# q and k projected in 32-column tiles and turned by VectorE, exp per head from PSUM, rotary tables scaled ahead, layernorm sums on half arrays

## The chip, the cores and the metric

The kernel runs on one core of one Trainium2 chip. The core has TensorE (PE) for matrix products, VectorE (DVE), ScalarE (ACT) and GpSimd (POOL) for elementwise work, and SyncE (SP), which issues the transfers here. TensorE reads its operands from the on-chip memory SBUF and writes its products to PSUM, eight banks of 128 partitions by 512 float32. The metric is the device time of one execution in microseconds.

## The reference, cut to what matters

Input x has 2 sequences of 2048 tokens with 128 features. Four residual steps follow one another; each reads the layernorm of x.

```python
x = x + attn_a(ln(x))            # full attention, softmax over the first token axis
x = x + ffn(ln(x))               # two layers, below
x = x + attn_b(ln(x))            # token weights from q/k statistics and a small convolution
x = x + ffn(ln(x))

def layer(x, ...):               # ffn is two of these
    q, k, v = split(shift_token(x) @ wqkv, 3)      # 8 heads of 64
    q, k = l2norm(q) * q_scale, l2norm(k) * k_scale
    q = q * cos * scale + rotate_half(q) * sin * scale
    k = k * cos / scale + rotate_half(k) * sin / scale
    x = x + local_attention(q, k, v) @ wo          # windows of 64, each sees itself and the one before
    h = layernorm(shift_token(x)) * lg + lb
    a, g = split(h @ w1 + b1, 2)
    return x + (a * gelu(g)) @ w2 + b2
```

The windowed attention is run over 2 sequences, 2 uses of ffn, 2 layers and 16 blocks of 128 tokens: 128 blocks in all, each of 8 heads. All arithmetic is float32; only the mask is bfloat16.

## The kernel before

**How it is put together.** The kernel does not issue instructions directly. `op(engine, cost, fn, r, w, claim)` notes an operation with the engine that runs it, an assumed cost in microseconds, and what it reads and writes. `Program.run` then walks through a list schedule with these costs, hands out buffers from fixed pools (`sizes`, with the eight PSUM banks as pool `p1`), and issues the operations in the resulting order. That order is fixed on every engine; only semaphores decide when each instruction starts. So the costs in the code shape the order, and the chip sets the times.

**The stages.** Tokens are loaded in 8 chunks of 512. `first_norm` and `first_attention` do the full attention of each sequence. Then `Block.tick` runs the ffn steps: 16 blocks of layer 0, with layer 1 of the same sequence 6 ticks behind, the next sequence following. After every fourth block comes `feed_forward` on 512 tokens. `token_weights` does the third step of a sequence.

**A block of windowed attention** (`Attention.block`). The state `s` lies with features on partitions and tokens along the free axis. The steps with their lines:

- L498, L499: a table of 4 x 64 trigonometric values for each token is loaded, and POOL multiplies it by the q and k scales.
- L503: q and k are projected, each one product of 128 tokens by 512 columns into one PSUM bank; L507 does v. A float32 product is two passes in the profile. Tokens now lie on partitions.
- L510, L514: SP copies halves of v to a buffer with shifted windows.
- L523: ACT squares q and k; L524, L525: DVE multiplies them by the two halves of the table, the second with the halves of each head exchanged; L527: DVE sums the squares over each head.
- L528: POOL adds the two products. L530 to L533: POOL clips the sums of squares, ACT takes the inverse root by Ln and Exp, and `newton` refines it in four small POOL operations. L536: POOL multiplies the rotated q and k by it.
- L543, L545 (through `transposes`, L389): eight 128x128 transposes on TensorE bring features back to partitions; ACT copies q (L544) and k into a ring of three blocks (L546).
- L557, L573: scores of the two windows and two head parities, each in a 64x64 quadrant of the array. A masked bfloat16 product starts each sum.
- L581, L582: DVE takes the row maxima and subtracts them; L583: ACT takes the exponential of all 1024 columns; L587, L588: DVE sums rows and inverts; L593: POOL scales the weights.
- L600, L601: eight more transposes and their copies; L612: the product with v by 64-column tiles; L618: ACT copies; every second block, L624 projects the output and L630, L631 add it to the state.

**Layernorm** (`center`, L453 to L463) works on 128 features by 512 tokens. A product with `meanw`, a matrix of 1/128, puts the mean of each token on all 128 partitions (L457); DVE subtracts (L458), ACT squares, a second such product gives the variance (L460), and ACT takes the inverse root by Ln and Exp (L461, L462). It is called 56 times: 16 times by `state_norm`, 32 times by `feed_forward`, 8 times by `token_weights`.

## Time and profile before

| | us |
|---|---|
| median of three runs | 1736.16 |
| lowest and highest of them | 1735.68, 1736.17 |
| profiled execution | 1736.7 |
| span of its instructions | 1734.9 |

The mean granted TensorE clock of the profiled execution is 0.986. Line numbers (L503) are those of the kernel before. In a row of groups, the count after x is the number of records, and a group can be split by the buffer that its tile got. Busy time is the union of the instructions' times; the idle time is that of the engine just before the group's instructions. In a timeline, neighbouring instructions of one kind are merged into one row with their number. Some matmul records can be missing.

### The profile page before, as it was taken

Reading aid. Unit: us, or ns where it says so; the run is one execution under the profiler, and the core shown is the slowest. Engines: PE = TensorE matmul, PEld = TensorE weight load, DVE = VectorE, ACT = ScalarE, POOL = GpSimd, SP = SyncE. Lnnn points to the kernel's source line nnn. Section 1 sums busy time; section 2 is a strip of 40 time slices with the busy share of each in tenths; the row PEclk is TensorE's granted clock in tenths of the full one; section 3 lists DMA queues with packets and bytes.
Section 4 is the critical chain, followed back from the end, with each engine's and each line's share of the span. In section 5 each row is a group of like instructions: output and inputs, shape, how many; then the busy total and the mean of one; then the engine's idle time right before and its main releaser. Section 6 shows DMA issues by size and latency. Waiting matters only on the chain.

```text
span 1734.9 us, 35224 instructions
## 1 busy us (share of the span) xinstructions
PE 1660.6 (96%) x13638; PEld 996.6 (57%) x13638; DVE 1277.5 (74%) x2095; ACT 1112.4 (64%) x2029; POOL 1196.2 (69%) x1548
## 2 busy tenths in 40 slices
PE   8999998999999999899999998999999999999996
PEld 4444446665656565456666664565656665665654
DVE  6323258787778886888788797887788888888663
ACT  6444456666677666667766765767676776766663
POOL 4000029789788785688699686869699788987762
PEclk9999999999999999899999999999999999999998
DMA  5000001111111110111111111111111111111110
GB/s 156 0 0 1 0 22 41 32 41 41 37 29 44 38 26 22 31 29 40 35 38 41 32 26 31 32 35 38 38 41 44 44 43 44 33 49 40 32 32 7
DMA packets 50603, 59.98 MB, mean 35 GB/s; under 512 B 6955, under 2 KB 33925, under 8 KB 50437
## 3 DMA queue, kind: packets, MB, share of 16 engines
q1 hardware_dynamic: 50436, 57.73, 13.3%
q8 instruction: 108, 1.77, 0.4%
q14 instruction: 59, 0.48, 0.1%
HBM read 23.11 MB, written 2.10 MB: 15 GB/s over the span
## 4 chain that ended last, share of the span: by engine, by line
PE 67%; DVE 14%; POOL 13%; ACT 3%; issue 3%; DMA 0%; POOLq 0%; SPq 0%; DVEq 0%; ACTq 0%
PE pp L389 10%; PE pp L660 8%; PE pp L503 8%; PE pp L446 6%; PE pp L435 6%; PE pp L612 6%; PE pp L624 5%; PE pp L573 4%; PE pp L507 4%; PE pp L685 4%; POOL arena L528 3%; DVE b_m L581 2%; DVE arena L582 2%; POOL arena L593 2%; POOL arena L536 2%
## 5 line engine op out<-in xcount | busy, mean ns | idle before, releaser
L593 POOL TENSOR_TENSOR arena<-arena,b_m 128x512 f32<-128x512 f32 x226 | 230.3, 1040 | 102.1 <-DVE b_m L588 84.3
L389 PE MATMUL pp<-ident,arena 128*128 128x128 f32 x1792 | 250.8, 279 | 23.4 <-POOL arena L593 10.7
L389 PEld LDWEIGHTS pp<-ident,arena 128*128 128x128 f32 x1792 | 206.8, 143 | 112.8 <-issue 56.2
L503 PE MATMUL pp<-wqkv,b_s 128*128 128x512 f32 x512 | 258.2, 607 | 0.2 <-POOL b_s L483 0.2
L528 POOL TENSOR_TENSOR arena<-arena 128x1024 f32<-128x1024 f32 x90 | 212.6, 2364 | 29.9 <-DVE arena L525 27.9
L536 POOL TENSOR_TENSOR arena<-arena,b_n 128x1024 f32<-128x1024 f32 x107 | 203.8, 1906 | 3.1
L581 DVE TENSOR_REDUCE b_m<-pp 128x4 f32<-128x512 f32 x256 | 165.1, 679 | 47.0 <-PE pp L573 45.0
L660 PE MATMUL pp<-b_c,w 128*128 128x512 f32 (+1 forms) x384 | 179.5, 618 | 16.3 <-POOL b_c L656 10.9
L524 DVE TENSOR_TENSOR arena<-pp,b_tab 128x512 f32<-128x512 f32 x214 | 145.9, 683 | 61.4 <-ACT arena L523 33.3
L601 ACT COPY arena<-pp 128x512 f32<-128x512 f32 x232 | 130.0, 589 | 89.0 <-PE pp L389 83.8
L482 POOL TENSOR_TENSOR b_s<-b_c,b_c 64x512 f32<-64x512 f32 x16 | 20.3, 1266 | 210.5 <-ACT b_c L462 210.3
L523 ACT ACTIVATE arena<-pp 128x512 f32<-128x512 f32 x220 | 129.7, 598 | 46.9 <-PE pp L503 45.7
L612 PEld LDWEIGHTS pp<-arena,b_v 128*64 128x64 f32 x3712 | 119.7, 138 | 63.0 <-issue 21.7
L587 DVE TENSOR_REDUCE b_m<-arena 128x8 f32<-128x1024 f32 x113 | 137.0, 1213 | 23.9 <-ACT arena L583 23.3
L525 DVE TENSOR_TENSOR arena<-pp,b_tab 128x512 f32<-128x512 f32 x222 | 151.0, 680 | 0.3
L582 DVE TENSOR_TENSOR arena<-pp,b_m 128x512 f32<-128x512 f32 x226 | 147.4, 682 | 0.4
L583 ACT ACTIVATE arena<-arena 128x1024 f32<-128x1024 f32 x113 | 119.7, 1059 | 39.3 <-DVE arena L582 38.7
L527 DVE TENSOR_REDUCE b_n<-arena 128x16 f32<-128x1024 f32 x110 | 132.6, 1209 | 11.3 <-ACT arena L523 11.2
L612 PE MATMUL pp<-arena,b_v 128*64 128x64 f32 x3712 | 136.0, 226 | 2.8 <-ACT arena L601 2.6
L573 PE MATMUL pp<-kring,b_c 64*64 64x128 f32 x4096 | 136.6, 272 | 1.4 <-ACT kring L546 1.4
L507 PE MATMUL pp<-wqkv,b_s 128*128 128x512 f32 x256 | 134.4, 610 | 0.8 <-DVE arena L525 0.7
L660 PEld LDWEIGHTS pp<-b_c,w 128*128 128x128 f32 (+1 forms) x384 | 69.0, 184 | 114.3 <-issue 77.2
(195 smaller groups left out, 3238.5 us busy)
## 6 DMA issues: line engine op xcount, KB each, us to landing
b_v<-b_v SPq DMA_DIRECT2D x248, 128.0 KB, 2.2
b_tab<-in_rot_dram SPq DMA_DIRECT2D x128, 128.0 KB, 2.1
b_c<-in_x_dram SPq DMA_DIRECT2D x8, 256.0 KB, 4.7
out_dram<-b_c SPq DMA_DIRECT2D x8, 256.0 KB, 2.3
wqkv<-in_wqkv_dram SPq DMA_DIRECT2D x1, 1536.0 KB
w<-in_w_dram SPq DMA_DIRECT2D x1, 682.0 KB, 5.0
wo<-in_wo_dram SPq DMA_DIRECT2D x2, 256.0 KB, 8.9
masks<-in_masks_dram SPq DMA_DIRECT2D x1, 384.0 KB, 8.7
```

What stands on the lines that cost most here:

```text
L389: pe_.transpose(pt()[:, k * P : (k + 1) * P], at(k), ident)
L503: op("PE", pe(512), lambda k=k: pe_.matmul(out=pq[k](), lhsT=h(), rhs=wqkv[:, l, k * INNER : (k + 1) * INNER], start=True, stop=True), r=k ...
L507: op("PE", pe(512), lambda: pe_.matmul(out=pv(), lhsT=h(), rhs=wqkv[:, l, 2 * INNER : 3 * INNER], start=True, stop=True), r=keys_of(s, q) ...
L525: op("DVE", dve(512), lambda heads=heads, src=src, trig=trig: dv.tensor_tensor(heads(t2), src()[:, :, ::-1, :], trig(1), ALU.mult), r=[pq[ ...
L528: op("POOL", pool(1024), lambda: po_.tensor_tensor(t1(), t1(), t2(), ALU.add), r=[t2], w=[t1])
L536: lambda: po_.tensor_tensor(t1().rearrange("p (h d) -> p h d", d=DH), t1().rearrange("p (h d) -> p h d", d=DH), nr()[:, 0:16].unsqueeze(2) ...
L573: pe_.matmul(out=o.rearrange("p (n c) -> p n c", c=WIN), lhsT=q_, rhs=k, start=False, stop=(pair == 3))
L581: op("DVE", dve(512), lambda sim3=sim3, mx=mx: dv.tensor_reduce(mx(), sim3(), AX.X, ALU.max, negate=True), r=[sim[par]], w=[(nm, par)])
L582: op("DVE", dve(512), lambda sim3=sim3, mx=mx, p4=p4: dv.tensor_tensor(p4(), sim3(), mx().unsqueeze(2).to_broadcast([P, 4, P]), ALU.add), ...
L593: lambda hs=hs: po_.tensor_tensor(p3()[:, hs, :], p3()[:, hs, :], rs()[:, hs].unsqueeze(2).to_broadcast([P, 4, P]), ALU.mult),
L612: pe_.matmul(out=av()[par * 64 : par * 64 + 64, pair * P + w * WIN : pair * P + (w + 1) * WIN], lhsT=(v if w else v0)()[:, hd * DH : (hd + ...
L660: op("PE", pe(512), lambda: pe_.matmul(out=p_()[0:n, :], lhsT=w1[:, l, off + j * P : off + j * P + n], rhs=d(), start=True, stop=True), r= ...
```

## The change

**Layout of q and k.** The columns of `wqkv` are reordered on the host, so that a block's q and k are made in four groups of features. Each product has 32 tokens as its stationary columns and 256 columns of weights, and writes 32 partitions: partition group c of the result holds feature group c, and the four token groups lie along the free axis. `project(k)` issues 8 such products in place of one. A feature group has 16 features of the first half of a head and their 16 partners of the second half, so that the exchange of halves happens within 32 columns. Tables, scales and masks follow the new layout; the mask is stored once and repeated by its access pattern.

```diff
+            def project(k):
+                for a in range(2):
+                    for c in range(4):
+                        at = q * P + (2 * k + a) * 32
+                        pe_.matmul(out=pq[k]()[c * 32 : c * 32 + 32, a * 256 : (a + 1) * 256], lhsT=s()[:, at : at + 32], rhs=wqkv[:, l, c * 256 : (c + 1) * 256], start=True, stop=True, tile_position=(0, c * 32))
+
             for k in range(2):
-                op("PE", pe(512), lambda k=k: pe_.matmul(out=pq[k](), lhsT=h(), rhs=wqkv[:, l, k * INNER : (k + 1) * INNER], start=True, stop=True), ...)
+                op("PE", pe(512), lambda k=k: project(k), r=keys_of(s, q) + [wqkv_], w=[pq[k]], claim=[sq, t1, t2])
```

**Norms.** A head's 64 features now lie on two partition groups. The sums of squares are taken over 32 columns (32 sums for each partition in place of 16), a product with the 128x128 matrix `twin` adds the two partner groups, and the clip moves from POOL to DVE[...]. Adding the two rotary products, POOL reads the second with its halves of 16 exchanged.

```diff
-            op("DVE", dve(1024), lambda: dv.tensor_reduce(nv()[:, 0:16], sq().rearrange("p (h d) -> p h d", d=DH), AX.X, ALU.add), r=[sq], w=[nv])
-            op("POOL", pool(1024), lambda: po_.tensor_tensor(t1(), t1(), t2(), ALU.add), r=[t2], w=[t1])
-            op("POOL", 0.22, lambda: po_.tensor_scalar(nv()[:, 0:16], nv()[:, 0:16], 1e-24, None, ALU.max), w=[nv])
+            nv, nr, pn = buf("n"), buf("n"), buf("p1")
+            op("DVE", dve(1024), lambda: dv.tensor_reduce(nv()[:, 0:32], sq().rearrange("p (h d) -> p h d", d=32), AX.X, ALU.add), r=[sq], w=[nv])
+            op("PE", 0.25, lambda: pe_.matmul(out=pn()[:, 0:32], lhsT=twin, rhs=nv()[:, 0:32], start=True, stop=True), r=[nv, twin_], w=[pn])
+            op("DVE", 0.2, lambda: dv.tensor_scalar(nv()[:, 0:32], pn()[:, 0:32], 1e-24, None, ALU.max), r=[pn], w=[nv])
+            halves = lambda t: t().rearrange("p (n s d) -> p n s d", s=2, d=16)
+            op("POOL", pool(1024), lambda: po_.tensor_tensor(halves(t1), halves(t1), halves(t2)[:, :, ::-1, :], ALU.add), r=[t2], w=[t1])
```

**Turning.** In place of eight TensorE transposes and two ACT copies, two DVE transposes exchange rows and columns within 32x32 squares, from SBUF to SBUF.

```diff
-            pt = transposes(4, t1, lambda k: t1()[:, k * P : (k + 1) * P], qT)
-            op("ACT", act(512), lambda pt=pt: ac.copy(qT(), pt()), r=[pt], w=[qT])
-            pt = transposes(4, t1, lambda k: t1()[:, (4 + k) * P : (5 + k) * P])
-            op("ACT", act(512), lambda pt=pt: ac.copy(ring[:, :, slot * P : (slot + 1) * P], ...), r=[pt], w=[(ring_, slot)])
+            tq = lambda k: t1().rearrange("p (a k n d) -> p a k n d", a=4, k=2, n=4)[:, :, k]
+            to = lambda o: o.rearrange("p n (a d) -> p a n d", a=4)
+            op("DVE", dve(512), lambda: dv.transpose(to(qT().rearrange("p (n d) -> p n d", n=4)), tq(0)), r=[t1], w=[qT])
+            op("DVE", dve(512), lambda: dv.transpose(to(ring[:, :, slot * P : (slot + 1) * P]), tq(1)), r=[t1], w=[(ring_, slot)])
```

**Exponential.** DVE no longer subtracts the row maximum. For each head, ACT reads 128 columns of the scores from PSUM and takes the exponential with the negated maximum as its bias: eight instructions in place of one.

```diff
-                op("DVE", dve(512), lambda ...: dv.tensor_tensor(p4(), sim3(), mx().unsqueeze(2).to_broadcast([P, 4, P]), ALU.add), ...)
-            op("ACT", act(1024), lambda: ac.activation(p(), p(), AF.Exp), w=[p], act="E")
+                def weights(par=par):
+                    for k in range(4):
+                        hd = par * 4 + k
+                        ac.activation(p()[:, hd * P : (hd + 1) * P], sim[par]()[:, k * P : (k + 1) * P], AF.Exp, bias=nm()[:, hd : hd + 1])
+
+                op("ACT", 4 * 0.29 + 0.1, weights, r=[sim[par], (nm, par)], w=[(p, par)], act="E")
```

**Tables.** `tables()`, called after the first sequence's `first_norm`, loads each of the 16 tables (now 512 columns), has POOL multiply it by the scales of each layer, and stores the 32 results in device memory. A block loads its finished table.

```diff
+    def tables():
+        for i in range(NBLK):
+            raw = buf("tab")
+            op("SP", 0.1, lambda i=i, raw=raw: sp.dma_start(out=raw(), in_=I["rot"][i]), w=[raw])
+            for l in range(DEPTH):
+                tab = buf("tab")
+                op("POOL", 1.3, lambda ...: po_.tensor_tensor(...), r=[raw, qs_], w=[tab])
+                op("SP", 0.1, lambda l=l, i=i, tab=tab: sp.dma_start(out=turns[l][i], in_=tab()), r=[tab], w=[turns_[l][i]])
...
-            op("SP", 0.1, lambda: sp.dma_start(out=tab(), in_=I["rot"][i]), w=[tab])
-            op("POOL", 0.75, lambda: po_.tensor_tensor(tab(), tab(), qs[:, l], ALU.mult), r=[(qs_, l)], w=[tab])
+            op("SP", 0.1, lambda: sp.dma_start(out=tab(), in_=turns[l][i]), r=[turns_[l][i]], w=[tab])
```

**Layernorm.** The sums are taken with 64 columns of `meanw`: the first 256 tokens go to partitions 0 to 63, the others to 64 to 127, side by side in one bank. DVE then subtracts in four pieces of 64 partitions by 256 tokens. Ln works on 256 columns, and Exp writes its result in four pieces.

```diff
+        half = [slice(0, 64), slice(64, 128)]
+        toks = [slice(0, CH // 2), slice(CH // 2, CH)]
+        def sums(o, of):
+            for t in range(2):
+                pe_.matmul(out=o()[half[t], toks[0]], lhsT=meanw[:, 0:64], rhs=of()[:, toks[t]], start=True, stop=True)
+        op("PE", pe(256), lambda: sums(mp, src), r=keys, w=[mp], claim=[d, sq])
+        for t in range(2):
+            for f in half:
+                op("DVE", dve(256), lambda t=t, f=f: dv.tensor_tensor(d()[f, toks[t]], src()[f, toks[t]], mp()[half[t], toks[0]], ALU.subtract), ...)
...
+        op("PE", pe(256), lambda: sums(vp, sq), r=[sq], w=[vp], claim=[r])
```

**Buffers.** The hidden layer (`h`) and `token_weights`' normalised input (`y`) are made of 512-column buffers of pool `c`, which grows from 11 to 18 as pools `h` and `y` go; pool `v` grows from 5 to 6.

## The prediction

> **What bounds it now.** I read first the busy line of the page, then the granted clock, then the busy times by stretch, then TensorE's own timeline, and last the costliest groups.
>
> ```profile
> span 1734.9 us, 35224 instructions
> ...
> PE 1660.6 (96%) x13638; PEld 996.6 (57%) x13638; DVE 1277.5 (74%) x2095; ACT 1112.4 (64%) x2029; POOL 1196.2 (69%) x1548
> ...
> PE 67%; DVE 14%; POOL 13%; ACT 3%; issue 3%; DMA 0%; POOLq 0%; SPq 0%; DVEq 0%; ACTq 0%
> ```
>
> TensorE is busy 96% of the span; the chain of waits runs through it for 67%, and no DMA is on it. The busy times by stretch, in the order PE, PEld, DVE, ACT, POOL, clock, DMA share, say where:
>
> ```profile
> 0.00:350.00 350.00, 335.22 (x1505) 171.51 (x1506) 177.82 (x368) 181.98 (x366) 109.66 (x177) 0.99 0.11 32
> 350.00:1600.00 1250.00, 1210.05 (x11090) 753.39 (x11089) 1021.53 (x1607) 856.70 (x1540) 1010.31 (x1283) 0.99 0.15 37
> 1600.00:1735.00 135.00, 115.38 (x1048) 71.71 (x1046) 78.19 (x122) 73.72 (x124) 76.28 (x90) 0.95 0.10 23
> ```
>
> The first 350 us hold the full attention, which the change hardly touches. The rest, 1385 us, is the block part: TensorE 1325 us, DVE 1100, POOL 1087, ACT 930. So 60 us of TensorE idle there (4.3%), and its nearest follower, DVE, carries 83% of TensorE's load. A microsecond off TensorE counts until DVE stands beside it.
>
> A matmul's duration overlaps its neighbours', so I price TensorE by distances between starts:
>
> ```profile
> 1403.87 1.02 PE L503 MATMUL pp<-wqkv,b_s 128*128 128x512 f32 x2
> 1404.83 0.41 PE L557 MATMUL pp<-masks,identb 64*64 64x512 bf16 x4
> 1405.07 1.04 PE L573 MATMUL pp<-kring,b_c 64*64 64x128 f32 x32
> 1405.94 0.39 PE L557 MATMUL pp<-masks,identb 64*64 64x512 bf16 x4
> 1406.15 1.04 PE L573 MATMUL pp<-kring,b_c 64*64 64x128 f32 x32
> 1407.13 1.09 PE L389 MATMUL pp<-ident,arena 128*128 128x128 f32 x8
> 1408.06 1.02 PE L507 MATMUL pp<-wqkv,b_s 128*128 128x512 f32 x2
> 1408.92 0.60 PE L389 MATMUL pp<-ident,arena 128*128 128x128 f32 x4
> ```
>
> Three prices. A full 512-column f32 product is two passes: 1408.06 to 1408.92, 0.86 us. Score tiles: 32 passes of 128 columns take 0.87 us (1405.07 to 1405.94); one such pass alone lasts a quarter of 0.43, 0.107, so 32 in a row would take 3.4 us: four 64x64 tiles run abreast. And a change of tile shape: the first L503 pair needs 0.96 to the 64x64 masks, the second score set 0.98 to the full-array transposes, against 0.86 and 0.87 with no change: 0.10 per change.
>
> **TensorE, part by part.**
> 1. *Turning of q and k leaves TensorE.* 8 of a block's 16 transposes go, 1024 in 128 blocks. Eight at L389 take 1407.13 to 1408.06, 0.93, less one shape change of 0.10 is about 0.11 each: **-112 us**.
> 2. *q, k by 32-column tiles.* A half becomes 8 products of 256 columns, 16 passes. A 256-column pass takes half of 0.43, 0.215. Four column tiles abreast make 4 rounds of 0.215 = 0.86, as now. No row has 128x32 tiles abreast, so two ends: +0 (the scores' four abreast), or two abreast, 8 rounds, 1.72, +0.86 x 256 = +220 us. Nearest rows: the scores (four), and L612, 128 rows by 64 columns, two abreast: 32 passes of 64 columns in 1.08 us less a shape change (1412.97, an L507 following at 1414.05 in the timeline), 0.98, where perfect pairs give 16 x 0.054 = 0.86. That loss is some 7 ns a round; four rounds in 256 halves make +7. I take **+4**.
>    A rule speaks against this: the Trainium skill, "TensorE: Matmul & The Clock Gate", Part 3 (Measured speedup vs the span model), gives three 32-column tiles as 2.38 times one after another, not 3. At that efficiency, 79%, a half takes 0.86/0.79 = 1.09, +0.23 x 256 = +58 us by the rule, against +4 by the rows. I take the rows: that figure is of one pack, with its fill and end inside, while the scores here are a stream and lose nothing.
> 3. *Shape changes.* Counted in the two programs as built, TensorE's tile shape changes 482 times before and 845 after: 363 x about 0.095 = **+34**.
> 4. *The sum over twin partitions* is a product with 128x128 weights and 32 columns, two passes. Not shown; below is 2 x 0.027 for the columns, above two full weight loads (L389 loads 128 columns each 0.11): 0.05 to 0.22. Weights bind, so 0.20 x 128 = **+26**.
> 5. *Layernorm sums.* 56 normalisations (112 rows at L457, two passes each) with two products of 0.86; each becomes two 256-column products side by side, 0.43: 112 x 0.43 = **-48** (their shape changes are in 3).
>
> Sum: -112 + 4 + 34 + 26 - 48 = **-96 us** of TensorE, 1325 to 1229.
>
> **The other engines**, which decide how much of that arrives.
>
> ```profile
> L582 DVE TENSOR_TENSOR arena<-pp,b_m 128x512 f32<-128x512 f32 x226 | 147.4, 682 | 0.4
> ...
> L583 ACT ACTIVATE arena<-arena 128x1024 f32<-128x1024 f32 x113 | 119.7, 1059 | 39.3 <-DVE arena L582 38.7
> ...
> L499 POOL TENSOR_TENSOR b_tab<-b_tab,qs 128x256 f32<-128x256 f32 x128 | 93.2, 730 | 1.7 <-DMA b_tab<-in_rot_dram 0.6 <-POOL b_s L471 0.2
> ...
> L437 ACT ACTIVATE arena<-pp,b_n 128x512 f32<-128x512 f32 x64 | 44.0, 687 | 14.2 <-PE pp L435 12.3 <-POOL b_m L381 1.1
> ...
> L630 DVE TENSOR_TENSOR b_s<-pp,b_s 64x256 f32<-64x256 f32 x64 | 26.3, 411 | 23.2 <-PE pp L624 23.0
> ```
>
> The columns are busy time, mean ns of one, idle before and its releasers. Back to back, DVE starts are some 0.08 us nearer than a duration (two at L582 take 1.28, not 1.36), ACT's some 0.1.
>
> *DVE.* The two subtractions of the row maximum go: 256 x 0.60 = -154. Two 128x512 transposes come. No row has one. Below, a plain 512-column operation, 0.60 each, +154. Above: the skill's "VectorE: DVE Perf Modes", The three transpose paths, has 311 ns for 128x128 in bf16; four of these are 1.24, +318, 164 us more than the rows. "Vector Engine (DVE) Microarchitecture Reference", The reshape front-end, says one element per cycle per lane, which is L582's rate, and the 311 holds a fixed part that is paid once here. I take 0.60: 0 net. The clip moves here from POOL: the reciprocal at L588, 0.20 less 0.08, and a little for PSUM: 0.15 x 128 = +19. A layernorm subtraction of 0.60 becomes four of 64x256, 0.34 each by L630: +0.76 x 56 = +43. **DVE +60**, 1100 to 1160.
>
> *ACT.* A block's exp goes (1.06 less 0.1) and so do two copies (0.5 each); eight exps of 128 columns come: L437's 0.687 less 384 columns at 0.84 ns (L583's 1059 ns against 631 for 512 columns at L459) is 0.37, 0.27 back to back, 2.15. Net +0.2 x 128 = +25; the layernorm's Ln on half arrays and four exps +0.55 x 56 = +30. 930 to 985: no bound.
>
> *POOL.* The scaling at L499 goes (-93) and the clip (-32). 32 scalings of 512 columns, about 1.3 each by L656's 1.27, come early, where POOL is busy 110 of 350 us: hidden, and were they late, the first blocks would wait. The sum of the two rotary products reads runs of 16 in reverse; L528 has 2.36 for plain rows: I take no change; a quarter more would be +75 on 960 and still hidden.
>
> *DMA.* A block's table is 256 KB instead of 128, 16 loads and 32 stores are added on SP; its share is 0.15 in the blocks. On SP the added work stands before the blocks; a block's load waits for its stored table, written long before, and for a free buffer as now, and the copies of v stand behind it. DVE loses the 33 us it waits for L499. Hidden. Masks by broadcast, h and y in smaller buffers: no instruction more, 0.
>
> **What arrives.** After, DVE carries 1160 beside TensorE's 1229, 94% instead of 83%: two engines in a fixed order, each now stalling the other. Were TensorE's idle share to stay 4.3%, the block part is 1229/0.957 = 1284, the span 1634. With 10% idle it is 1366, 1716. I choose 6.5%: 1229/0.935 = 1314, **span 1664**. The profiled run took 1736.7 for its span of 1734.9, and stands 0.5 over the median: **1666 us**.
>
> **Rivals.**
> - *DVE becomes the bound*, 0.18. Its clip waits for the twin product in TensorE's queue, and behind it on DVE stand maxima, row sums and the next block's rotary products, for which ACT and POOL wait. At 0.6 us a stall, 128 x 0.6 = 77, or at 0.9 us a transpose the same: DVE 1237, at 92% of the time 1345, 350 + 1345 + 2 = 1697; both, 1730. For it: between 1400 and 1600 us DVE is busy 170.6 of 200. Against: 82% over the long stretch above.
> - *Column tiles don't run four abreast*, 0.11: **slower**. At two abreast +220 on 1666 is 1886. It decides from 70/256 = 0.27 more per half, a round of 0.28 instead of 0.215, three abreast. For it: four moving streams over all 128 rows are nowhere in the trace, the scores have two per row. Against: the small loss at L612.
> - *TensorE's saving arrives whole*, 0.08: waits for tables and PSUM copies vanish too, 1634 and below, about 1620.
> - *Nothing to see*, 0.04: the saved transposes are paid back by stalls, 1736.
>
> The likeliest has 0.59 (1630 to 1695). What this kernel's measurement can tell from no change is about 0.2%, 3.5 us. Range **1620 to 1735**: without the tile case, the no-change case's upper half and the far side of the first. Faster 0.83, same 0.04, slower 0.13 (tile case and a stall worse than priced).
>
> **What would show it.** Right: L389's transposes at 1120, TensorE busy near 1560, starts of a q/k half some 0.86 apart plus 0.1 for the shape change, DVE transposes near 0.68, DVE idle behind the twin product small. Wrong: 16 passes in 1.1 us or more; DVE above 90% with TensorE waiting for it at the scores; POOL's rotary sum well over 2.4 us.

## The result: half a per cent, and the profile after

| | us |
|---|---|
| before, median | 1735.93 |
| after, median of four runs | 1726.9 |
| lowest and highest of them | 1725.94, 1727.55 |
| ratio, 95% interval | 0.9948 [0.993, 0.9965] |
| span of the profiled execution, before and after | 1734.9, 1724.2 |
| mean granted TensorE clock, before and after | 0.986, 0.974 |

The change made the kernel faster, inside the range, but by 9 us in place of the 70 forecast. The page of the kernel after, its first lines and the chain of waits (whose record breaks off after 1% of the span, so that it says nothing here):

```profile
span 1724.2 us, 42427 instructions
...
PE 1600.9 (93%) x16678; PEld 931.7 (54%) x16678; DVE 1357.1 (79%) x2391; ACT 1170.5 (68%) x2837; POOL 1131.5 (66%) x1324
...
PE 1%; ACT 0%; DVE 0%; issue 0%; POOLq 0%; DVEq 0%; ACTq 0%
```

TensorE is busy 60 us less than before and the span is only 11 us shorter. The busy times by stretch of the kernel after (columns as before: PE, PEld, DVE, ACT, POOL, granted clock, DMA share, GB/s):

```profile
0.00:350.00 350.00, 330.11 (x1794) 165.83 (x1794) 182.67 (x387) 183.60 (x413) 135.64 (x178) 0.99 0.23 72
350.00:1600.00 1250.00, 1174.48 (x13946) 708.96 (x13945) 1106.76 (x1893) 918.11 (x2269) 937.86 (x1084) 0.98 0.19 49
1600.00:1724.20 124.20, 96.30 (x941) 56.92 (x939) 67.70 (x113) 68.79 (x155) 58.05 (x64) 0.92 0.10 25
```

The block part is 1374 us long, TensorE is busy 1271 of it and idle 103, or 7.5%. The forecast had 1229 busy and 85 idle (6.5%). So of the 60 us that are missing, **42 are TensorE time and 18 are idle time**. DVE (1174 in the block part, forecast 1160) and ACT (987, forecast 985) came out as worked out.

The groups of the kernel after, each shape apart (busy time, mean ns of one, idle before and releasers):

```profile
L552 PE MATMUL pp<-wqkv,b_s 128*32 128x256 f32 x4096 | 268.8, 392 | 6.3 <-DVE b_s L752 2.2 <-DVE b_n L582 0.8 <-ACT arena L639 0.8
L639 ACT ACTIVATE arena<-pp,b_m 128x128 f32<-128x128 f32 x872 | 242.4, 390 | 63.9 <-DVE b_m L634 59.5 <-POOL b_n L385 1.5 <-POOL arena L651 0.7
L584 POOL TENSOR_TENSOR arena<-arena 128x1024 f32<-128x1024 f32 x93 | 220.2, 2368 | 24.0 <-DVE arena L577 22.5 <-PE pp L394 0.9
L483 ACT ACTIVATE b_c<-arena 64x256 f32<-64x256 f32 x196 | 81.5, 416 | 2.4
L599 DVE STREAM_TRANSPOSE b_c<-arena 128x512 f32<-128x512 f32 x111 | 77.2, 695 | 11.6 <-POOL arena L590 11.1
L600 DVE STREAM_TRANSPOSE kring<-arena 128x512 f32<-128x512 f32 x111 | 74.8, 674 | 0.2
L474 DVE TENSOR_TENSOR b_c<-b_s,pp 64x256 f32<-64x256 f32 x128 | 53.6, 418 | 10.0 <-PE pp L469 6.4 <-issue 0.8
```

The transposes on VectorE last 0.67 to 0.70 us and the rotary sum with exchanged halves 2.37, as forecast. L474 and L483, the layernorm's pieces, will matter below: eight such instructions stand where two stood.

What TensorE waits for, in the kernel before and in the kernel after (us in total, times, longest):

```profile
PE pp L660 <- POOL b_c L656: 10.9, 7, 2.8
PE pp L389 <- POOL arena L593: 10.7, 16, 2.0
PE pp L389 <- POOL arena L536: 6.9, 5, 2.9
...
PE pp L460 <- ACT arena L459: 2.2, 2, 1.4
```

```profile
PE pp L394 <- POOL arena L651: 18.4, 20, 4.5
PE pp L469 <- ACT arena L475: 16.3, 12, 3.0
PE pp L718 <- POOL b_c L714: 9.7, 6, 3.7
PE pp L581 <- DVE b_n L580: 7.0, 5, 3.7
PE pp L627 <- DVE kring L600: 6.1, 6, 3.2
```

L394 holds the transposes (L389 before), L651 the scaling of the weights (L593 before), L469 both layernorm sums (L457 and L460 before), L475 the square between them (L459 before). The wait of the second layernorm sum for the square has grown from 2.2 us to 16.3 (from 2.8 to 20.5 with the other buffer that the square can lie in): it has grown the most, and it lies in a part of the change that was to save TensorE 48 us.

One such wait, in the timeline of the kernel after, with all engines in order of time (start, duration, engine, line, operation, tiles, count merged, idle before):

```profile
1036.07 0.65 PE L469 MATMUL pp<-b_s,meanw 128*64 128x256 f32 x4
1036.58 1.21 DVE L580 TENSOR_REDUCE b_n<-arena 128x32 f32<-128x1024 f32 x1
1036.65 1.07 PE L552 MATMUL pp<-wqkv,b_s 128*32 128x256 f32 x16
1037.70 1.74 DVE L474 TENSOR_TENSOR b_c<-b_s,pp 64x256 f32<-64x256 f32 x4
...
1039.54 0.63 ACT L475 ACTIVATE arena<-b_c 128x512 f32<-128x512 f32 x1 [1.03 <-DVE b_c L474]
...
1040.22 1.12 PE L469 MATMUL pp<-arena,meanw 128*64 128x256 f32 x4 [2.50 <-ACT arena L475]
...
1043.71 3.33 PE L552 MATMUL pp<-wqkv,b_s 128*32 128x256 f32 x32
```

The first sum is done at 1036.7. DVE, busy with a block's reduction, takes up the four pieces at 1037.70 and needs 1.74 us, where the one subtraction of before lasts 0.68; then ACT squares, and TensorE stands for 2.50 us. The two q/k halves after it take 3.33 us in place of some 1.9. The windows of the same place, with the granted clock in the third column from the right, show why:

```profile
1033.00:1036.40 3.40, 3.40 (x30) 1.46 (x28) 3.31 (x7) 1.76 (x4) 3.07 (x7) 1.00 0.02 5
1036.40:1039.80 3.40, 1.32 (x20) 0.42 (x16) 3.29 (x7) 2.31 (x6) 3.32 (x3) 1.00 0.44 110
1039.80:1046.60 6.80, 6.38 (x36) 2.61 (x40) 4.95 (x9) 4.10 (x10) 5.09 (x5) 0.50 0.20 60
```

After a stretch in which TensorE was busy 1.3 of 3.4 us, the clock was granted at 0.50 for 6.8 us, so the wait was paid for twice. Of the 17 stretches at half clock in this trace, 15 follow a 3.4 us window in which TensorE was idle for 1.7 to 3.3 us; before the other two it was not idle. Counted from the other side, on the grid of 3.41 us on which the clock's changes lie: of 16 windows at full clock with 1.75 us of idle time or more, 15 were followed by half clock, and of 28 with 1.0 to 1.7 us none. That is this trace's border and no general one: in e18 below, half clock follows less than 0.7 us three times. Over the span the clock that was not granted is 1724.2 x 0.026 = 45 us after, 1734.9 x 0.014 = 24 before.

**TensorE's account.** It sums the distances between the starts of successive matmuls in each trace; its terms hold to some 4 us. "Columns" is what the passes need at full clock (0.43 us for 512 columns; 0.107 for a full-array pass of 128 columns or fewer, for which loading 128 columns of weights sets the time: the twin product's passes of 32 columns take 0.12 each; tiles side by side share it); "changes" is the time over that, which is tile-shape changes and gaps under 0.2 us; "half clock" is the excess inside windows granted at half; "idle" the gaps shown as idle. In us:

| | columns | changes | half clock | idle |
|---|---|---|---|---|
| before | 1512 | 125 | 23 | 66 |
| after | 1382 | 176 | 42 | 115 |
| after less before | -130 | +51 | +19 | +49 |

"Columns" is a count of passes times a price. That it comes near the forecast's -134 (-112 + 26 - 48) says that no pass was forgotten, not that the passes took what was forecast. Of these 130 us, 119 came back in the three other terms.

Line by line, the same distances (idle time and what half clock adds left out) are measurements: the transposes fell by 112 us, as forecast, and the layernorm sums by 39 in place of 48; q and k rose by 19, the twin product took 35, and v took 11 more, since the tile shape changes behind it 76 times in place of 17.

### The profile page after: what moved, and what is told of

Its sections match the earlier page's. It is cut to its first block, busy times and chain, and to the rows that moved or that the text cites. A ratio compares the mean times of both kernels' runs of the same rounds, so it can differ in the third digit from the quotient of the medians.

```text
span 1724.2 us, 42427 instructions
## 1 busy us (share of the span) xinstructions
PE 1600.9 (93%) x16678; PEld 931.7 (54%) x16678; DVE 1357.1 (79%) x2391; ACT 1170.5 (68%) x2837; POOL 1131.5 (66%) x1324
## 5 line engine op out<-in xcount | busy, mean ns | idle before, releaser
L651 POOL TENSOR_TENSOR arena<-arena,b_m 128x512 f32<-128x512 f32 x218 | 222.2, 1040 | 123.8 <-DVE b_m L646 90.3
L639 ACT ACTIVATE arena<-pp,b_m 128x128 f32<-128x128 f32 x872 | 242.4, 390 | 63.9 <-DVE b_m L634 59.5
L552 PE MATMUL pp<-wqkv,b_s 128*32 128x256 f32 x4096 | 268.8, 392 | 6.3 <-DVE b_s L752 2.2
L718 PE MATMUL pp<-b_c,w 128*128 128x512 f32 (+1 forms) x384 | 179.8, 618 | 10.7 <-POOL b_c L714 9.7
L552 PEld LDWEIGHTS pp<-wqkv,b_s 128*32 128x32 f32 x4096 | 115.2, 111 | 120.8 <-issue 40.2
L394 PE MATMUL pp<-ident,arena 128*128 128x128 f32 x904 | 136.1, 286 | 26.3 <-POOL arena L651 18.4
L659 ACT COPY arena<-pp 128x512 f32<-128x512 f32 x208 | 118.7, 602 | 58.2 <-PE pp L394 51.4
L559 PE MATMUL pp<-wqkv,b_s 128*128 128x512 f32 x256 | 142.2, 641 | 6.0 <-DVE arena L577 2.9
L394 PEld LDWEIGHTS pp<-ident,arena 128*128 128x128 f32 x904 | 104.9, 146 | 73.1 <-POOL arena L651 34.5
L580 DVE TENSOR_REDUCE b_n<-arena 128x32 f32<-128x1024 f32 x115 | 138.1, 1202 | 0.1
L627 PEld LDWEIGHTS pp<-kring,b_c 64*64 64x64 f32 x4096 | 122.9, 135 | 16.6 <-DVE kring L600 8.1
L670 PE MATMUL pp<-arena,b_v 128*64 128x64 f32 x3328 | 124.4, 228 | 3.3 <-ACT arena L659 3.3
```

What stands on the lines that cost most here:

```text
L394: pe_.transpose(pt()[:, k * P : (k + 1) * P], at(k), ident)
L552: pe_.matmul(out=pq[k]()[c * 32 : c * 32 + 32, a * 256 : (a + 1) * 256], lhsT=s()[:, at : at + 32], rhs=wqkv[:, l, c * 256 : (c + 1) * 256 ...
L627: pe_.matmul(out=o.rearrange("p (n c) -> p n c", c=WIN), lhsT=q_, rhs=k, start=False, stop=(pair == 3))
L639: ac.activation(p()[:, hd * P : (hd + 1) * P], sim[par]()[:, k * P : (k + 1) * P], AF.Exp, bias=nm()[:, hd : hd + 1])
L651: lambda hs=hs: po_.tensor_tensor(p3()[:, hs, :], p3()[:, hs, :], rs()[:, hs].unsqueeze(2).to_broadcast([P, 4, P]), ALU.mult),
L670: pe_.matmul(out=av()[par * 64 : par * 64 + 64, pair * P + w * WIN : pair * P + (w + 1) * WIN], lhsT=(v if w else v0)()[:, hd * DH : (hd + ...
```

## The experiments

All times are medians; "before" ran on the same chips at 1736 to 1740. The order of the instructions comes from the scheduler's prices, so every edit below also moves other instructions about; three runs (e7, e11, e12) price that.

**e1, the changed kernel with the layernorm on full arrays**, and **e2, the changed kernel with the old exponential** (DVE subtracts, one ACT instruction):

```diff
# e1, against after
-        op("PE", pe(256), lambda: sums(mp, src), r=keys, w=[mp], claim=[d, sq])
-        for t in range(2):
-            for f in half:
-                op("DVE", dve(256), lambda t=t, f=f: dv.tensor_tensor(...), ...)
+        op("PE", pe(512), lambda: pe_.matmul(out=mp(), lhsT=meanw, rhs=src(), start=True, stop=True), ...)
+        op("DVE", dve(512), lambda: dv.tensor_tensor(d(), src(), mp(), ALU.subtract), ...)
...
# e2, against after
-                op("ACT", 4 * 0.29 + 0.1, weights, r=[sim[par], (nm, par)], w=[(p, par)], act="E")
+                op("DVE", dve(512), lambda ...: dv.tensor_tensor(p4(), sim3(), mx()..., ALU.add), ...)
+            op("ACT", act(1024), lambda: ac.activation(p(), p(), AF.Exp), w=[p], act="E")
```

> The changed kernel with the layernorm part undone (full-array sums, one subtraction, one Exp). Undoing moves DVE by about -58 us (four pieces took 92.8 by distances between starts, one took 35.1), ACT by -50, TensorE by +28 (+48 of columns, -20 of shape changes). Theory 1, DVE's load sets how much of TensorE's saving arrives: 1690 to 1710 us, faster than the changed kernel's 1727. Theory 2, TensorE's own work sets the time: 1727 + 28 = 1755. Theory 3, the new chain of the norms and turns (twin product, clip, transposes) holds TensorE up: little moves, 1720 to 1740.

> The changed kernel with the exponential undone (DVE subtracts the maxima, ACT takes 1024 columns at once). DVE +154 us, ACT -138, TensorE 0. Theory 1 (DVE's load): DVE 1357 + 154 = 1511, beyond TensorE's work in the block part, 1800 to 1850 us. Theory 2 (TensorE's own work): 1720 to 1740. Theory 3 (chain of norms and turns): 1730 to 1760, since the row maxima's path gets longer too.

Measured: e1 1715.64, ratio 0.9868 [0.9847, 0.989]; e2 1790.95, ratio 1.0305 [1.0277, 1.0332]. Without the layernorm part the kernel is 11 us faster than with it. Without the exponential part it is 64 us slower: with the transposes on DVE and the subtraction too, DVE is busy 1503 us, and TensorE idle 158. The change without this part is slower than the kernel before.

**e3, before with everything but the turning** (exponential, tables, layernorm), and **e4, before with the exponential alone**: the same diffs put into the kernel before.

> The kernel before with the exponential per head, the tables scaled ahead and the layernorm on half arrays, but q and k projected and transposed as before. Against before: TensorE -28 us, DVE -154 + 58 = -96, POOL -93 in the blocks, ACT +138 + 50 - 0 = +188. Theory 1: DVE has room, TensorE is the bound with less idle, 1685 to 1705 us. Theory 2: 1736 - 28 = 1708. Theory 3: 1685 to 1705, and the turning part alone is then a loss of 20 us or more in the changed kernel.

> The kernel before with the exponential per head alone: DVE -154 us, ACT +138, TensorE 0. All theories: TensorE keeps its 1660 us of busy time; the 66 us of its idle time are what can go. Theory 1: 1705 to 1725. Theory 2 and 3: 1725 to 1740, as DVE was not what TensorE waited for (24 us of its idle ended on DVE).

Measured: e3 1744.42, 1.0043 [1.0028, 1.0057]; e4 1728.24, 0.9947 [0.9925, 0.9968]. The exponential alone has the ratio of the whole change; with tables and layernorm added the gain is lost.

**e5 and e6, is DVE the bound?** e5 leaves out the row sums: each is replaced by the first weight plus 1, and DVE drops from 1357 to 1272 us busy. e6 is e1 with the row sums of one head parity taken by ACT's accumulator; DVE drops from 1298 to 1235.

```diff
# e5, against after
-            op("DVE", dve(1024), lambda: dv.tensor_reduce(rs()[:, 0:HEADS], p3(), AX.X, ALU.add), r=[p], w=[rs])
+            op("DVE", 0.2, lambda: dv.tensor_scalar(rs()[:, 0:HEADS], p3()[:, :, 0], 1.0, None, ALU.add), r=[p], w=[rs])
...
# e6, against e1
-                        ac.activation(p()[:, hd * P : (hd + 1) * P], sim[par]()..., AF.Exp, bias=nm()[:, hd : hd + 1])
+                        ac.activation(p()..., sim[par]()..., AF.Exp, bias=nm()[:, hd : hd + 1], **(dict(accum_out=rs()[:, hd : hd + 1]) if par else {}))
```

> The changed kernel without its row sums: it leaves out the sum of the weights of each head (DVE, 1.13 us a block) and takes the first weight plus one in its place (about 0.1 us), after the same exponentials. DVE falls by about 133 us to 1224, TensorE, ACT and POOL keep their work. Theory 1 (DVE's load decides how much of TensorE's saving arrives): 1670 to 1695 us. Theory 3 (the longer chains of the layernorm and the norms hold TensorE up, whatever DVE's load): 1712 to 1727, only what the shorter softmax path brings. Theory 4 (the order is wrong since its costs are): 1700 to 1727.

> The kernel of full-array layernorm (1715.6) with the row sums of one head parity taken by ACT's accumulator: DVE -74 us to about 1224, ACT +98 (four accumulator reads of 0.19 a block) to 1217, TensorE the same. Theory 1: 1690 to 1705 us. Theory 3: 1710 to 1725, as the exponentials of that parity end later.

Measured: e5 1725.21, 0.9928 [0.9913, 0.9942]; e6 1721.03, 0.9901 [0.988, 0.9922]. With 85 us off DVE the time stands still, and e6 is 5 us slower than e1. The page of e5, beside the 1357.1 of the kernel after:

```profile
PE 1611.4 (94%) x16678; PEld 933.7 (54%) x16678; DVE 1272.5 (74%) x2391; ACT 1164.4 (68%) x2837; POOL 1133.4 (66%) x1324
```

The changed kernel does not follow DVE's total load downwards. Each is one order, so a gain of 10 or 20 us could hide, but hardly the 32 to 57 us that the theory of DVE's load had for e5. (e2, with 146 us more on DVE and a longer chain in each block, was 64 us slower.)

**e7, e11, e12, the order alone.** e7 is the changed kernel with 0.05 to 0.15 us more for the TensorE steps that change the tile shape in the scheduler's prices; e12 has every column priced 2% higher; e11 is the kernel before with that nudge. No instruction differs.

```diff
# e7, against after
-                op("PE", pe(512), lambda k=k: project(k), ...)
+                op("PE", pe(512) + 0.1, lambda k=k: project(k), ...)
-        op("PE", pe(256), lambda: sums(mp, src), ...)
+        op("PE", pe(256) + 0.15, lambda: sums(mp, src), ...)
...
# e11 against before, e12 against after
-    return cols / 592.0
+    return cols / 580.0
```

> The changed kernel with only the scheduler's costs mended by what the trace shows: a half of q or k +0.1 us, the twin product 0.34, each layernorm sum +0.15, four transposes +0.05, the product with v +0.05. The work is the same, its order differs. Theory 4 (the order is wrong since its costs are): 1690 to 1710 us. Theories 1 and 3: 1715 to 1740, as any order of the same work.

> The kernel before with the scheduler's price of a TensorE column raised by 2% and nothing else: the same work in a slightly different order. It measures what an order is worth. Theory 3 and theory 1 as stated so far take an order for neutral: within 0.3% of before, 1732 to 1743. If an order alone is worth as much as e7 showed: up to 1720 or 1760.

> The changed kernel with the same 2% on TensorE's columns and nothing else. Within 0.3% of the changed kernel, 1722 to 1732, if an order is neutral; 1705 to 1750 if order alone moves it as in e7, and then differences of 10 us between variants of this study are not read as the worth of a part.

Measured: e7 1746.35, 1.0049 [1.0034, 1.0064], 19 us above the kernel after; e11 1750.42, 1.0063 [1.0048, 1.0078]; e12 1720.04, 0.9889 [0.9871, 0.9906]. The same instructions in another order are worth -7 to +19 us against the order they came in. The intervals of the runs are far narrower: they are of one order each. So a difference of 10 us between two versions in one order each is not yet a cost of the edit, and e1's 11 us, e4's gain and the 9 us of the change itself are of that size.

**e8, before with the layernorm alone; e9, before with full sums but its subtraction and Exp in four pieces; e15, the subtraction's pieces alone.** In e9 and e15 TensorE does exactly what it did before.

```diff
# e9, against before (e15 has the first half of it)
-        op("DVE", dve(512), lambda: dv.tensor_tensor(d(), src(), mp(), ALU.subtract), r=keys + [mp], w=[d])
+        for t in range(2):
+            for f in half:
+                op("DVE", dve(256), lambda t=t, f=f: dv.tensor_tensor(d()[f, toks[t]], src()[f, toks[t]], mp()[f, toks[t]], ALU.subtract), ...)
-        op("ACT", act(512), lambda: ac.activation(r(), r(), AF.Exp, scale=-0.5), w=[r], act="E")
+        def roots():
+            for t in range(2):
+                for f in half:
+                    ac.activation(r()[f, toks[t]], r()[f, toks[t]], AF.Exp, scale=-0.5)
+        op("ACT", 4 * (act(256) - 0.1) + 0.1, roots, w=[r], act="E")
```

> The kernel before with the layernorm on half arrays alone: TensorE -48 us of columns and about +22 of shape changes, DVE +58 to 1335, ACT +50. Theory 2 (TensorE's own work): 1710 us. Theory 1: 1715 to 1735, DVE is then at 77%. Theory 3 (TensorE waits for the longer layernorm chain): 1740 to 1755, with TensorE's idle time ending on ACT's square and POOL's product of the layernorm.

> The kernel before with the layernorm's full-array sums kept and only its vector work cut up: the subtraction in four pieces of 64 partitions by 256 tokens, the Exp in four pieces. TensorE's work and tile shapes are those of before; DVE about +58 us, ACT about +60, and each layernorm takes some 2 us longer. Theory 3 (TensorE waits for the longer layernorm chain): 1760 to 1790 us, the 1759 of the layernorm part alone plus the 26 us that TensorE saved there. Theory 2: 1737. Rival 5, that it was the tile shapes and not the chain: 1735 to 1745.

> The kernel before with only the subtraction in four pieces, Exp whole: the chain is longer by about 1.07 us, DVE +58, ACT 0. If both halves of the cut count by their length (1.07 of 2.2 us): about half of e9's +46, 1755 to 1768. If the Exp pieces, last before POOL's product and behind ACT's queue, carry it: 1738 to 1750.

Measured: e8 1759.4, 1.0126 [1.0107, 1.0145]; e9 1785.07, 1.0257 [1.024, 1.0274]; e15 1776.31, 1.0225 [1.0206, 1.0243]. Pieces alone cost 46 us, those of DVE alone 40, against before on the same chip; that is twice what order alone was seen to do. The 48 us of columns that the half arrays save get back about half of it, and the part remains a loss of 22 us. (These 22 alone are not clear of the order: e11 is 12 us slower than before without any edit.) In e15, its busy line and TensorE's waits:

```profile
PE 1678.3 (95%) x13638; PEld 996.4 (56%) x13638; DVE 1331.3 (75%) x2263; ACT 1116.3 (63%) x2029; POOL 1191.4 (67%) x1548
```

```profile
PE pp L389 <- POOL arena L541: 13.3, 9, 3.2
PE pp L665 <- POOL b_c L661: 10.6, 9, 3.1
PE pp L464 <- ACT arena L463: 8.7, 11, 2.6
PE pp L464 <- ACT b_w L463: 3.3, 2, 2.2
```

L464 is the second layernorm sum and L463 the square: 2.8 us before in both buffers, 12.0 here, though TensorE has the same work. That is nearly half of the 21 us by which its idle time grew. The wait is long wherever the subtraction is cut (e9 12.6, e8 18.0, after 20.5), and short where it is whole (e18 4.8). The first row, a block's transposes behind POOL's scaling of the rotated q and k (L536 before, 6.9), has doubled too.

**e13 and e16, is it only the wrong price?** The scheduler took a piece at 0.34 us on DVE and 0.29 on ACT. e13 is e9, e16 the changed kernel, with 0.08 more for a DVE piece and 0.415 for an ACT piece.

```diff
-                op("DVE", dve(256), lambda t=t, f=f: dv.tensor_tensor(...), ...)
+                op("DVE", dve(256) + 0.08, lambda t=t, f=f: dv.tensor_tensor(...), ...)
-        op("ACT", 4 * (act(256) - 0.1) + 0.1, roots, ...)
+        op("ACT", 4 * 0.415 + 0.1, roots, ...)
```

> The kernel of e9 (pieces alone, 1785) with only the scheduler's price of the pieces mended by the trace: a piece of the subtraction 0.42 us and of the Exp 0.415 between starts, where the schedule counted 0.34 and 0.29. Theory 3a, the chain is longer whatever the order: 1770 to 1790. Theory 3b, the order was made for a chain that is 0.9 us too short, and TensorE's fixed queue meets it too early: 1735 to 1760.

> The changed kernel with only the price of the pieces mended as in e13. Theory 3b: 1690 to 1715, as the order then leaves room for the layernorm's chain. Theory 3a: 1715 to 1740, no more than another order of the same work.

Measured: e13 1771.72, 1.0193 [1.0169, 1.0217], so 11 of the 46 us go and 35 stay, each against before on its own chip; e16 1718.12, 0.9895 [0.9875, 0.9915], 9 us below the kernel after. Both moves are of the size of the order's.

**e14, the pieces beside the chain.** The kernel before keeps its one subtraction and one Exp; three more DVE pieces and three more ACT pieces of the same size are computed into scratch that nobody reads.

```diff
+        for t, f in more:
+            op("DVE", dve(256), lambda t=t, f=f: dv.tensor_tensor(sq()[f, toks[t]], d()[f, 0 : CH // 2], d()[f, CH // 2 : CH], ALU.subtract), r=[d], w=[(sq, (t, f.start))])
...
+        def again():
+            for t, f in more:
+                ac.activation(sq()[f, toks[t]], r()[f, 0 : CH // 2], AF.Exp, scale=-0.5)
+        op("ACT", 3 * (act(256) - 0.1) + 0.1, again, r=[r], w=[(sq, "again")], act="E")
```

> The kernel before with the same extra load as e9 but beside the layernorm's chain: the subtraction and the Exp stay whole, and three more pieces of each engine (64x256, results not used) stand behind them, for which nobody waits. DVE about +70 us, ACT about +70, the chain as before. If it is the length of the chain (3a, 3b): 1735 to 1750. If it is the load and the queues of DVE and ACT: 1770 to 1790, like e9.

Measured: 1811.55, ratio 1.0424 [1.0402, 1.0446], 75 us more, and worse than e9. The run was to tell a longer layernorm chain from fuller queues of DVE and ACT. Its trace shows that it can't, for two reasons. The pieces are not of e9's size:

```profile
PE 1690.5 (93%) x13638; PEld 997.9 (55%) x13638; DVE 1415.1 (78%) x2263; ACT 1181.5 (65%) x2197; POOL 1210.1 (67%) x1548
```

```profile
L465 DVE TENSOR_TENSOR arena<-b_c 64x256 f32<-64x256 f32 x147 | 122.2, 833 | 4.2
```

DVE is busy 138 us more than before, where e9 has it busy 60 more. These pieces take both operands from SBUF, e9's one of them from PSUM. At the median one lasts 0.42 us, but 66 of the 168 last over 0.55 and up to 2.6: each of these 66 began while a POOL instruction ran, and ended 0.28 us after that or a later one.

And the pieces are not beside the chain. In `feed_forward` POOL multiplies `d` by the inverse root in place (L667), so it has to wait until the pieces have read `d`:

```profile
POOL b_c L667 <- DVE arena L465: 11.9, 17, 1.4
```

In 25 of its 32 executions the product starts some 0.14 us after the end of a DVE piece, with the Exp that it needs done 0.4 to 2.8 us before. So e14 makes the chain longer too, at its other end. TensorE's waits that grew stand behind POOL:

```profile
PE pp L389 <- POOL arena L547: 19.3, 14, 4.2
PE pp L671 <- POOL b_c L667: 17.3, 15, 3.2
PE pp L389 <- POOL arena L604: 15.0, 19, 4.1
```

L547 is the scaling of the rotated q and k (L536 before, 6.9), L604 the scaling of the weights (L593, 10.7), L667 the product in the feed-forward (L656, 10.9). POOL is the last link, with the same 1548 instructions as before.

**e10, before with exponential and tables.**

> The kernel before with the exponential per head and the tables scaled ahead, layernorm and turning as before; beside the kernel of full-array layernorm (1715.6) it shows the turning of q and k alone. POOL -93 us in the blocks, DVE -154, ACT +138, TensorE 0. If the turning part pays as TensorE's account says (-82 of columns, +20 of shape changes): 1735 or more is excluded by the exponential alone (1728), so 1715 to 1728, and the turning is worth 0 to 12. If the turning is a loss: below 1710.

Measured: 1724.78, ratio 0.9912 [0.9897, 0.9927]. That is 3 us below e4, less than an order does. e3 differs from e10 by the layernorm part alone and is 20 us slower. From e10 to e1 the turning is added, with its layout, norms and buffers: 9 us, again no more than an order does, where TensorE's columns fall by 82.

**e17 and e18, the layernorm on full arrays in two more orders.** e17 is e1 with the prices of e12, e18 is e1 with those of e7. With e1 they make three pairs that differ by the layernorm part alone, each pair in its own prices.

```diff
# e18, against e1
-        op("PE", 0.115 * n, run, r=[src, ident_], w=[pt], claim=dst)
+        op("PE", 0.115 * n + 0.05, run, r=[src, ident_], w=[pt], claim=dst)
-                op("PE", pe(512), lambda k=k: project(k), ...)
+                op("PE", pe(512) + 0.1, lambda k=k: project(k), ...)
-            op("PE", 0.25, lambda: pe_.matmul(out=pn()[:, 0:32], lhsT=twin, ...), ...)
+            op("PE", 0.34, lambda: pe_.matmul(out=pn()[:, 0:32], lhsT=twin, ...), ...)
-            op("PE", 1.1, combine, ...)
+            op("PE", 1.15, combine, ...)
```

> The changed kernel with the layernorm on full arrays, in another order: the scheduler's price of a column is 2% higher, no instruction differs from e1. Compare with e12, the changed kernel in the same nudge (1720). Theory A (the half-array layernorm costs time within the changed kernel, whatever the order): below e12 as e1 is below the changed kernel, 1705 to 1713. Theory B (e1's 11 us are luck of the order): anywhere from 1715 to 1735, and not below e12 by more than 3 us.

> As e17, but with the scheduler's prices of e7: 0.05 to 0.1 us more for the TensorE steps that change the tile shape, no instruction differs from e1. Compare with e7 (1746). Theory A: 1715 to 1738, at least 8 us below e7. Theory B: within 5 us of e7, or above it.

| prices | half arrays | full arrays | difference |
|---|---|---|---|
| as in the changed kernel (after, e1) | 1726.9 | 1715.64 | -11 |
| 2% a column (e12, e17) | 1720.04 | 1702.75 | -17 |
| shape changes priced (e7, e18) | 1746.35 | 1699.01 | -47 |
| of the kernel before, on it alone (e8, before) | 1759.4 | 1737.15 | -22 |
| the same, with exponential and tables (e3, e10) | 1744.42 | 1724.78 | -20 |

In the three pairs, and in the two that the earlier runs add, the layernorm part is a loss; the theory of a lucky order, as it was put on record, falls. How large the loss is stays open: e16, a fourth order of the half arrays at 1718.12, is only 2.5 us above e1. **e18 is the best version of all, 1699.01 us, ratio 0.9764 [0.9744, 0.9784]** (e17: 0.9788 [0.9767, 0.9809]): the change without its layernorm part, and with the shape changes in the prices. Its busy times by stretch:

```profile
0.00:350.00 350.00, 333.48 (x1832) 166.45 (x1832) 180.68 (x381) 183.56 (x412) 140.85 (x185) 1.00 0.24 73
350.00:1600.00 1250.00, 1208.91 (x13938) 725.79 (x13936) 1063.22 (x1764) 890.00 (x2153) 950.95 (x1097) 0.99 0.20 50
1600.00:1698.20 98.20, 77.50 (x696) 44.05 (x692) 48.82 (x80) 48.37 (x104) 40.82 (x44) 0.92 0.07 18
```

The block part is 1348 us with TensorE busy 1286, idle 4.6%, nearly the share of before (4.3%). Against the kernel after it has 48 us more columns, and only some 15 us more TensorE time. The accounts of the runs that decide, as above:

| | columns | changes | half clock | idle |
|---|---|---|---|---|
| before | 1512 | 125 | 23 | 66 |
| e15, pieces of the subtraction | 1512 | 133 | 33 | 87 |
| e14, pieces beside the chain | 1512 | 140 | 38 | 114 |
| after | 1382 | 176 | 42 | 115 |
| e7, after in another order | 1382 | 182 | 54 | 117 |
| e1, full layernorm | 1430 | 164 | 33 | 78 |
| e18, full layernorm, other order | 1430 | 168 | 22 | 70 |

## Why the prediction was wrong in size

**The step that failed is "What arrives": 1229 us of TensorE at 6.5% idle.** Measured in the same stretch: 1271 at 7.5%. It was wrong in both factors, and mostly in the first. The term behind most of it is the layernorm part: forecast as a saving of 48 us of TensorE's time, measured as a loss of 11, 17 and 47 us in three pairs of kernels.

- *TensorE's sum, -96.* Its count of passes held (-134 forecast, -130 by the account's prices). Its other terms were too small or missing. Changes of tile shape and the short gaps with them came to +51, where the sum had 34 + 4 (the traces have the 363 more changes that it counted, but at some 0.14 each, not 0.095). The clock was taken as fixed: 19 us more were lost at half clock, mostly behind waits, and the sum had no term for it. And 5 us of the saving fell into the first 350 us, which the forecast left as they were. 4 + 13 + 19 + 5 = 41 of the 42 us.
- *The layernorm part, -48 on TensorE, DVE +43 and ACT +30 at no price.* It costs more than its columns save, in three orders within the changed kernel (11, 17 and 47 us) and on the kernel before (22 and 20 us). The forecast charged DVE and ACT for the pieces only through their total load, in the choice of 6.5%. The runs speak against that on both sides: 85 us of DVE's busy time taken away elsewhere bring nothing that shows (e5), and 54 us put on it at the layernorm (1277.5 to 1331.3 busy) cost 40 (e15). Nearly half of e15's added idle time is TensorE waiting for the square, which is the layernorm's own chain made longer by the pieces. How the rest arises is not shown, as e14 does not tell the chain from the queues.
- *The size of a piece.* The subtraction's pieces were taken at 0.34 "by L630", its 0.41 less the overlap of two rows at L582. In the trace of after the pieces follow one another at a median of 0.437 for a duration of 0.418, ACT's at 0.427 for 0.416: no overlap at all. So DVE gains 4 x 0.437 - 0.60 = 1.15, times 56 = 64 us, not 43. The timeline of the kernel before had the row, which the forecast passed over: two instructions of this kind in a row, L630 and L631,

```profile
828.11 0.42 DVE L630 TENSOR_TENSOR b_s<-pp,b_s 64x256 f32<-64x256 f32 x1 [0.43 <-PE pp L624]
828.54 0.43 DVE L631 TENSOR_TENSOR b_s<-pp,b_s 64x256 f32<-64x256 f32 x1
```

  0.43 apart. The Trainium skill has a rule for this, "VectorE: DVE Perf Modes", Two Vector instructions with no wait between them: an instruction that starts in another quadrant (a group of 32 partitions) than the last one is held until the earlier ones have finished. The pieces alternate between partitions 0 and 64, and the rows agree with it. That it is the start partition and not the size was not tried; pieces in the order of their halves would tell.
- *Column tiles four abreast, +4 by the rows against +58 by the rule.* The rows were right. In the kernel after 32 passes at L552, two halves, start at 1029.84 and the next instruction at 1031.70:

```profile
1029.50 0.41 PE L581 MATMUL pp<-b_n,twin 128*128 128x32 f32 x2
1029.84 1.93 PE L552 MATMUL pp<-wqkv,b_s 128*32 128x256 f32 x32
1031.70 1.56 PE L682 MATMUL pp<-arena,wo 128*128 128x256 f32 x6
```

  1.86 less a shape change of 0.1 is 0.88 for a half, against the 0.87 forecast. The slower rival, two or three abreast, falls.
- *Turning off TensorE, -112.* The row's 0.93 for eight transposes has no change of shape in it, so taking 0.10 off was a wrong reading; with 0.116 each it would have been -119. The lines of the transposes fell by 112 all the same.
- *Twin product, 0.20 a block.* 1029.84 less 1029.50 is 0.34 with a shape change in it, so 0.24; right to 5 us in all.
- *Turning on DVE, 0.60 each against 1.24.* The transposes start 0.625 apart. The rows were right, and right were the exps too (0.249 between starts, 0.27 taken), POOL's rotary sum (no change) and the DMA (hidden: the only DMA wait of TensorE is that of the first load of x, 4.9 us after and 4.2 before).
- *The rival "DVE becomes the bound", 1697 to 1730.* Its upper end does not follow from its own terms: with both stalls DVE has 1314 us, which at the rival's 92% is 1428 and a span near 1780. Its time was nearest, by luck, since its mechanism was not it: with DVE's load lowered by 85 us nothing came (e5), and the stalls were not at its place, the twin product, where TensorE waits 7.0 us for DVE and DVE 12.8 for TensorE (L582). The stalls were at the layernorm sums and behind POOL's scaling of the weights.
- *What the forecast would have been without the layernorm part.* By its own terms -112 + 4 + 26 and the 289 more shape changes that the traces of before and e18 show, 27 at 0.095: -55, so 1270 us of TensorE, at the old idle share 4.3% a span of 350 + 1327 = 1677, at 6.5% 1708. Measured were spans of 1714, 1701 and 1698 (e1, e17, e18): between these ends or a little above, where the forecast with the layernorm part missed by 60 us.

**What stays open.** Why an order suits one version and not another: the same price of shape changes cost the changed kernel 19 us and gave the one with full layernorm 17. So 10 us of any of these differences can be order. The worth of the turning, the tables and the buffers is open for the same reason: none was tried in more than one order of both the version with it and the version without, and the buffers not by themselves. Beyond the wait for the square, the runs don't show by which waits the pieces cost their 40 to 46 us; pieces that neither lengthen the chain nor read two operands from SBUF would tell. That work taken off the same queue elsewhere brings nothing because nobody waits there is argued from e5 and e6, not shown.

## What to carry to other kernels

An engine with spare time is not free: 54 us of work on DVE cost 40 us at one place here, and 85 us taken off it at another brought nothing. So price an edit at its place, by who waits there, and not by the engine's total. Take the price of small pieces from two of the same kind in a row, and add to each wait of TensorE the half-clocked stretch that may follow it. Where a scheduler sets the order, test a part by undoing it in two or three orders, and put measured costs in the scheduler before judging the part. When an experiment puts work "beside" a chain, see in its trace how long that work takes there and who waits for it.

## What the runs showed of the hardware that was not expected

- Four float32 tiles of 128 rows by 32 columns lose next to nothing in a stream: 0.88 us for a half of 16 passes of 256 columns, where one full-array product takes 0.86.
- Float32 instructions of 64 partitions by 256 columns on alternating halves don't overlap, on DVE (0.437 between starts, 0.418 each) nor on ACT (0.427, 0.416), while 512-column ones on 128 partitions start 0.60 apart at 0.68 each and ACT's exps of 128 columns 0.249 apart at 0.39.
- A DVE instruction that reads two operands from SBUF can last until a POOL instruction is over: 66 of e14's 168 pieces, 0.42 us at the median, lasted over 0.55 us, and all of these ended 0.28 us after the end of a POOL instruction.
- A kernel whose TensorE is busy 93% of the span still met 17 stretches of 3.4 or 6.8 us at a clock of 0.50, 15 of them right after 1.7 to 3.3 us of idle time within 3.4 us.
